# Attention vectors spread by TensorE from 2 KB rows, a plan that knows the transfers' rate, leads by group, aggregates copied by ScalarE

## Chip, core and metric

The kernel runs on one core of one Trainium2 chip. The metric is the device time of one execution in microseconds; it is given as the median of several executions. The program computes everything in float32.

## What is computed

128 graphs of 128 nodes with 256 features each pass through three graph-attention layers and one gated graph layer. Before each of the four, the features are normalized per node and cut at zero; the layer's result is added to the features.

```python
h = jnp.maximum(_layernorm(x, axis=-1), 0.0)
# attention layer (three times, own W and a)
Wh = jnp.einsum('bnf,fo->bno', h, W)
e = (Wh @ a1)[:, :, None] + (Wh @ a2)[:, None, :]
e = jnp.where(e > 0, e, ALPHA * e)
attention = jax.nn.softmax(jnp.where(adj > 0, e, NEG_BIG), axis=-1)
x = x + jax.nn.elu(jnp.einsum('bij,bjo->bio', attention, Wh))   # the third times nodemask
# gated layer, three steps
m = jnp.einsum('bnd,de->bne', h, weight[i])
aggr = jnp.einsum('bst,bsd->btd', A, m)
h = _gru_cell(aggr, h, w_ih, w_hh, b_ih, b_hh)                  # r, z, n gates of 256 each
```

## The kernel before

**Groups.** The graphs are worked on in 33 groups: a first and a last one of two graphs, and 31 of four (`SIZES`). For each group `gat(g)` does the three attention layers and `gru(g, ...)` the three gated steps. Names carry the group, then the layer or step, then the half: `ahp_2_1_0` is group 2, second attention layer.

**The plan.** Nothing is issued while the Python code runs through the groups. Each call of `add(engine, cost, rank, fn, ...)` notes an operation with an estimate of its cost; `load` notes a DMA on SP. `Plan.issue` then schedules all of them on paper: at each turn it takes the operation that can start first by the estimates (among those within 0.1 us the one of the lowest rank), and no operation whose rank is more than 6 above the lowest unfinished one. The order so found is the order in which every engine's queue holds its instructions. Each engine works through its queue in this order, so an instruction that has to wait holds up all behind it. Before the change, each load has one number, `lands`, for the time from its issue to its landing, whatever else is in flight.

**Ranks.** Group g's gated steps have ranks 3g, 3g + 1 and 3g + 2; its attention layers begin at 3g - lead(g) and are 2 apart. `lead` decides how far ahead of its gated steps a group's attention is worked on: 8.5 for the first two groups (`FAR = 2`), 6.5 for all others.

**Setup.** `attention_weights` folds a layer's vector `a` into its matrix: DVE multiplies each row of `w` with `a` and sums (L294), TensorE transposes the sums to all partitions (`vp`, L299), ScalarE copies them (`va`, L306). For this, `a` must lie in all 128 partitions: `ab` is loaded by a DMA that reads the 2 KB 128 times (L287). `transposed` loads and turns the GRU's weights (`whh`, `wih`, `gt`), and `combined` multiplies them (`wcp`).

**An attention layer** (`attention`): statistics on DVE (`st`, `mv`), the root on POOL (`rs`), the normed features on ScalarE (`xn`), scores on DVE (`scr`, L505), masked sums `em` (L547), exponentials on ScalarE (L565), then the weights are turned (`atp` by TensorE for groups 0 and 1; through DRAM, `tr_at`, `d_at`, `at`, for the others, which also spread the second score through DRAM, `de`, `er`). TensorE multiplies: `ahp` (L617, 16 records of 128 columns for four graphs), copied to `ah` (L624), then `hp` (L636, 16 records of 256). The result goes by `t` (L650) and two DVE operations into `xo` (L652, L654).

**A gated step** (`step` in `gru`): TensorE makes the aggregate `agp` (L803) in two halves, from the node-major state `hn` and the adjacency `am`. A copy `ag` (L811, on DVE) brings each half to SBUF; the one PSUM bank of the tag `tr` is free again after it. The products `nn`, `r`, `z`, `ni` (all L780) read the state `h` and the weights `whh`, or `ag` and the combined weights `wc`. ScalarE makes `wn`, `r`, `n`, `z` (L833 to L853), DVE the new state `h` (L841 to L870). For groups 2 to 30 the state is brought into node-major form for the next step by a DVE transpose of 32 x 32 blocks, a store to DRAM and four loads (`tr_hn`, `d_hn`, `hn`); the other groups use TensorE transposes (`hnp`, L752). All groups but the first get their first `h` from the normed features `hn0` by such a transpose, store and loads (`tr_h`, `d_h`, `h`), and all but the last two bring their last state back so (`tr_o`, `d_o`, `o`).

A product of 512 columns in float32 stands in the profile as two records.

Of the kernel before, what the change touches and what calls it, by code (L numbers as in the profile page):

```python
# [39 lines left out]
class Plan:  # L40
# [12 lines left out]
    def val(self, pool, tag, bufs, make):  # L53
        return Val(self.rings.setdefault((id(pool), tag), [[None] * bufs, 0]), make)

    def load(self, lands, rank, fn, **keys):

        op = self.add("SP", 0.45, rank, fn, **keys)
        op.lands = lands
        return op  # L60

    def add(self, engine, cost, rank, fn, reads=(), writes=(), after=(), takes=()):
# [45 lines left out]
    def issue(self):  # L108
        waits_for = {op: len(op.deps) for op in self.ops}
        uses = {}  # L110
        for op in self.ops:
            for v in op.vals:
                uses[v] = uses.get(v, 0) + 1
        by_rank = sorted(self.ops, key=lambda op: op.rank)
        engines = sorted({op.engine for op in self.ops})
        ready, free = {e: [] for e in engines}, {e: 0.0 for e in engines}
        held = [op for op in self.ops if not op.deps]
        best, changed, low, order = {}, set(engines), 0, []

        def start(op):  # L120
            t = max(free[op.engine], op.ready)
            for v in op.vals:
                if not v.taken:
                    slots, n = v.ring
                    old = slots[n % len(slots)]
                    if old is not None:
                        if uses[old]:
                            return None
                        t = max(t, *(o.end + self.lag(o, op.engine, False) for o in old.ops))
            return t  # L130

        def choose(engine):
            found = [(start(op), op) for op in ready[engine]]
            found = [f for f in found if f[0] is not None]
            if not found:
                return None
            first = min(t for t, _ in found)
            soon = [(op.rank, t, i) for i, (t, op) in enumerate(found) if t <= first + self.WINDOW]
            _, t, i = min(soon)
            return t, found[i][1]  # L140

        while len(order) < len(self.ops):
            while by_rank[low].end is not None:
                low += 1
            limit = by_rank[low].rank + self.AHEAD
            for op in held:
                if op.rank <= limit:
                    ready[op.engine].append(op)
                    changed.add(op.engine)
            held = [op for op in held if op.rank > limit]  # L150
            for e in sorted(changed):
                best[e] = choose(e)
            changed = set()
            open_ = {e: best[e] for e in engines if best[e] is not None}
            assert open_, "the plan is stuck"
            e = min(open_, key=lambda e: open_[e][0])
            t, op = open_[e]
            ready[e].remove(op)
            op.end = free[e] = t + op.cost
            order.append(op)  # L160
            changed.add(e)
            for v in op.vals:
                uses[v] -= 1
                if not v.taken:
                    slots, n = v.ring
                    slots[n % len(slots)], v.ring[1], v.taken = v, n + 1, True
                    changed.update(engines)
                if not uses[v]:
                    changed.update(engines)
            for u in op.users:  # L170
                u.ready = max(u.ready, op.end + self.lag(op, u.engine, u.deps[op]))
                waits_for[u] -= 1
                if not waits_for[u]:
                    held.append(u)
        for op in order:
            for v in op.vals:
                v.t
            op.fn()
# [3 lines left out]
def kernel(  # L182
# [85 lines left out]

    ident = const.tile([P, P], FT, name="ident")
    make_identity(nc, ident)  # L270
    mhalf = const.tile([P, G], FT, name="mhalf")
    nc.vector.memset(mhalf, -0.5)

# [6 lines left out]
    def attention_weights(l, w, a):  # L280
        rank = 1.5 * l - 8.0
        wt, va = const_val(f"w_{l}", [KD, D]), const_val(f"va_{l}", [2, D])
        first = l - 11.2
        load(4.0, first, lambda: nc.sync.dma_start(
            wt.t, w.rearrange("(k p) o -> p k o", p=P)), writes=[wt])
        ab = val(su, "ab", [2, D], f"ab_{l}")
        load(4.0, first, lambda: nc.sync.dma_start(  # L287
            ab.t, bass.AP(tensor=a.tensor, offset=a.offset, ap=[[0, P], [1, 2 * D]])), writes=[ab])
        wa = val(su, "wa", [2, KD], f"wa_{l}")
        vp = bank("gat", f"vp_{l}")  # L290

        def one(s, k):
            scr = val(su, "scr", [D], f"scr_{l}_{k}_{s}")
            add("DVE", dve(D) + 0.08, rank, lambda: nc.vector.scalar_tensor_tensor(  # L294
                scr.t, wt.t[:, k, :], 1.0, ab.t[:, s, :], op0=OP.mult, op1=OP.mult,
                accum_out=wa.t[:, s, k : k + 1],
            ), reads=[wt, ab], writes=[scr, (wa, (s, k))])
            c = s * KD + k
            add("PE", 0.11, rank, lambda: nc.tensor.transpose(  # L299
                vp.t[:, c * P : (c + 1) * P], wa.t[:, s, k : k + 1].to_broadcast([P, P]), ident  # L300
            ), reads=[(wa, (s, k))], writes=[(vp, c)])

        for s in range(2):
            for k in range(KD):
                one(s, k)
        add("ACT", act(T), rank, lambda: nc.scalar.copy(  # L306
            va.t.rearrange("p s d -> p (s d)"), vp.t), reads=[vp], writes=[va])
        W.append(wt)
        VA.append(va)
# [6 lines left out]
    def mask():  # L316
        nm = val(su, "nm", [N], "nm")
        nmp = bank("gat", "nmp")
        load(8.0, SETUP, lambda: nc.sync.dma_start(nm.t[:B], nodemask), writes=[nm])
        add("PE", 0.11, SETUP, lambda: nc.tensor.transpose(nmp.t[:, :B], nm.t[:B], ident[:B, :B]),  # L320
            reads=[nm], writes=[nmp])
        add("ACT", act(P), SETUP, lambda: nc.scalar.copy(nmT.t, nmp.t[:, :B]),
# [5 lines left out]
    def transposed(src, dst, name):  # L328
        rows = src.shape[0] // P
        ld = val(su, "wld", [O3 // P, D], f"{name}_ld")  # L330
        load(8.0 if rows > KD else 4.0, SETUP, lambda: nc.sync.dma_start(
            ld.t[:, :rows], src.rearrange("(r p) d -> p r d", p=P)), writes=[ld])

        def part(k, r0, n):
# [53 lines left out]
    def load_bias(dst, src):  # L388
        def fn():
            with nc.allow_non_contiguous_dma(reason="768 biases, once"):  # L390
                nc.sync.dma_start(dst.t, src.rearrange("(c p) -> p c", p=P))
        add("SP", 0.8, SETUP, fn, writes=[dst])

    load_bias(bi, b_ih)
    load_bias(bh, b_hh)
# [32 lines left out]
    def exchanged(srcs, cut, dst, name, n, rank):  # L428
# [16 lines left out]

        for k in range(kd):
            blocks(k)
        load(2.8 if kd == 1 else 3.8, rank, lambda: nc.sync.dma_start(
            d.t.rearrange("q r j f -> (q r) j f"), tr.t[:, :, :f]), reads=[tr], writes=[d])

        def back(j):
            load(2.8 if kd == 1 else 3.8, rank, lambda: nc.sync.dma_start(
                dst.t[j * 32 : (j + 1) * 32, :, :f], d.t[:, :, j, :].rearrange("q r f -> r q f")
            ), reads=[d], writes=[(dst, j)])

# [3 lines left out]
    def turned_state(src, dst, name, n, rank):  # L459
# [6 lines left out]
        add("DVE", dve(n * P), rank, lambda: nc.vector.transpose(  # L466
            tr.t.rearrange("p b j -> p (b j)"), src.t[:, : n * P]
        ), reads=[src], writes=[tr], takes=[d, dst])
        load(2.6, rank, lambda: nc.sync.dma_start(d.t.rearrange("b p f -> p b f"), tr.t),
            reads=[tr], writes=[d])  # L470

        def back(j):
            load(2.8, rank, lambda: nc.sync.dma_start(
                dst.t[j * 32 : (j + 1) * 32, : n * P].rearrange("c (m r) -> c m r", r=32),
                d.t[:, :, j * 32 : (j + 1) * 32].rearrange("b (q c) r -> c (b q) r", q=Q),
            ), reads=[d], writes=[(dst, j)])
# [4 lines left out]
    def attention(g, l, xt, cap, xo):  # L481
# [40 lines left out]
        if far:  # L522
# [1 line left out]
                dram, f"de{n}", 2, lambda: dram.tile([P, n], FT, tag=f"de{n}", name=f"de_{name}")  # L524
            )
            er = val(gw, "er", [N * G], f"er_{name}")
            load(2.2, rank, lambda: nc.sync.dma_start(de.t, e.t[:, 1, :n]),
                reads=[(e, (1, b)) for b in range(n)], writes=[de], takes=[er, em])
            load(4.6, rank, lambda: nc.sync.dma_start(
                er.t[:, : N * n], de.t.rearrange("p n -> (p n)").partition_broadcast(P)  # L530
            ), reads=[de], writes=[er])
        else:
            e2 = bank("gat", f"e2_{name}")

# [125 lines left out]
    def gat(g):  # L660
# [3 lines left out]
        adj_t = val(grp, "adj", [G, N], f"adj_{g}", dtype=I32, cut=n)  # L664
        cap = val(grp, "cap", [G, N], f"cap_{g}", cut=n)
        am = val(grp, "am", [G, N], f"am_{g}", bufs=4, cut=n)
        load(4.8, rank - 4, lambda: nc.sync.dma_start(
            x0.t, x[b0 : b0 + n].rearrange("b n d -> n b d")), writes=[x0])
        load(4.8, rank - 3.6, lambda: nc.sync.dma_start(
            adj_t.t, adj[b0 : b0 + n].rearrange("b i j -> i b j")), writes=[adj_t])  # L670
        add("DVE", 0.42, rank, lambda: nc.vector.tensor_scalar(
            cap.t, adj_t.t, 0.0, 2.0 * BIG, op0=OP.is_gt, op1=OP.mult), reads=[adj_t], writes=[cap])
# [53 lines left out]
    def gru(g, xt, am, hn0, h0):  # L726
# [36 lines left out]
        def step(i):  # L763
# [22 lines left out]
            def aggregate(k):  # L786
# [21 lines left out]

                for b in range(n_g):
                    part(b)  # L810
                add("DVE", dve(TG), quick, lambda: nc.vector.tensor_copy(t.t[:, :TG], ps.t[:, :TG]),  # L811
                    reads=[ps], writes=[t])

            def half(c):
# [92 lines left out]

        for k in range(KD):
            result(k)
        load(2.6, rank, lambda: nc.sync.dma_start(  # L910
            out[b0 : b0 + n_g].rearrange("b n d -> n b d"), xt.t), reads=[xt])

    URGENT = 2.0

    def lead(g):

        return 8.5 if g < FAR else 6.5

    for g in range(NG):
        gru(g, *gat(g))  # L920
# [37 lines left out]
```

## Time and profile before

| What | Before |
|---|---|
| median of 3 runs | 2776.41 us (2775.74 to 2777.18) |
| profiled execution, whole | 2774.5 us |
| its span, first to last instruction | 2772.7 us |
| mean granted TensorE clock | 0.995 |
| TensorE (PE) busy | 2710.1 us, 98% |
| VectorE (DVE) busy | 2199.0 us, 79% |
| ScalarE (ACT) busy | 1171.7 us, 42% |
| DVE copies of aggregates (L811) | 198, of 128 x 512 mostly, 676 ns |
| loads of `ab` | 3, 256 KB each, 5.3 us to landing (first 16 us) |

In the profile's lines a group shows the line, the engine, the operation, the tiles as out<-in, the number of instructions, and after a bar busy time and mean duration. A wait shows who waited for whom, the total, the number of times and the longest. A row of the timeline shows its start and length in microseconds, and in brackets how long the engine was idle before it and who ended that. The granted clock is the share of TensorE's full clock that the chip allowed. SPq is SP's queue of DMA issues. An end of several waits is put down to the last of them.

### The profile page before, as it was taken

The page shows a single profiled execution, that of the slowest core. Times are in us where ns is not written, and L with a number is a line of the kernel's source. Part 1 is how long each engine was busy: PE and PEld are TensorE (multiplying, and loading weights), DVE is VectorE, ACT ScalarE, POOL GpSimd, SP SyncE. Part 2 cuts the span into 40 slices and gives each one's busy share as a digit, 9 for nine tenths or more (in the row PEclk, how much of TensorE's full clock was granted, in tenths as well). Part 3 has the DMA queues.
Part 4 walks back from the last instruction along what each step waited for, and adds up shares of the span by engine and source line. Part 5 has one row for each costly group of instructions (what it writes and reads, how often), then busy time and mean ns, then how long its engine had stood idle before and what let it go on. Part 6 is the DMA issues. An engine that isn't in the chain of part 4 may idle for free.

```text
span 2772.7 us, 32377 instructions
## 1 busy us (share of the span) xinstructions
PE 2710.1 (98%) x9557; PEld 1565.2 (56%) x9557; DVE 2199.0 (79%) x5738; ACT 1171.7 (42%) x2511; POOL 288.2 (10%) x369
## 2 busy tenths in 40 slices
PE   6998999999999999999999999999999999999998
PEld 4755555555555555555555555555555555555546
DVE  7778888887888878887888878788788887888644
ACT  4444444443444444443444444444344444444322
POOL 2101011010101010101011101011101010101000
PEclk9999999999999999999999999999999999999999
DMA  3213234333334323334333334333333333333310
GB/s 102 57 44 103 77 94 110 103 86 92 89 93 111 105 75 99 91 92 111 97 83 96 95 92 107 103 84 91 88 100 103 104 87 88 80 94 93 78 44 12
DMA packets 503519, 246.08 MB, mean 89 GB/s; under 512 B 280624, under 2 KB 472112, under 8 KB 503344
## 3 DMA queue, kind: packets, MB, share of 16 engines
q1 hardware_dynamic: 503344, 244.03, 33.6%
q8 instruction: 76, 1.25, 0.2%
q14 instruction: 99, 0.81, 0.1%
HBM read 140.06 MB, written 103.87 MB: 88 GB/s over the span
## 4 chain that ended last, share of the span: by engine, by line
PE 84%; DVE 11%; ACT 2%; DMA 1%; issue 1%; SPq 0%; POOL 0%; ACTq 0%; DVEq 0%; POOLq 0%
PE r L780 21%; PE z L780 21%; PE ni L780 11%; PE hp L636 10%; PE nn L780 9%; PE ahp L617 6%; PE agp L803 5%; DVE em L547 2%; DVE xo L652 1%; DVE xo L654 1%; ACT em L565 1%; DVE ag L811 1%; DVE d L867 1%; DVE h L870 1%; DVE d L863 1%
## 5 line engine op out<-in xcount | busy, mean ns | idle before, releaser
L780 PE MATMUL nn<-h,whh 128*128 128x512 f32 (+1 forms) x792 | 396.3, 582 | 11.2 <-DMA h<-d_h 9.0
L780 PE MATMUL r<-ag,wc 128*128 128x512 f32 (+1 forms) x792 | 394.5, 581 | 8.4 <-DVE ag L811 8.4
L780 PE MATMUL r<-h,whh 128*128 128x512 f32 (+1 forms) x792 | 395.2, 580 | 0.0
L780 PE MATMUL z<-h,whh 128*128 128x512 f32 (+1 forms) x792 | 394.3, 579 | 0.0
L780 PE MATMUL z<-ag,wc 128*128 128x512 f32 (+1 forms) x792 | 394.1, 579 | 0.0
L780 PE MATMUL ni<-ag,wc 128*128 128x512 f32 (+1 forms) x792 | 394.0, 579 | 0.0
L636 PE MATMUL hp<-w,ah 128*128 128x256 f32 x1536 | 360.5, 380 | 2.5 <-ACT ah L624 2.4
L636 PEld LDWEIGHTS hp<-w,ah 128*128 128x128 f32 x1536 | 290.5, 191 | 100.7 <-issue 61.5
L841 DVE SCALAR_TENSOR_TENSOR n<-r,wn 128x512 f32<-128x512 f32 (+1 forms) x198 | 133.6, 675 | 224.8 <-ACT r L838 222.9
L505 DVE SCALAR_TENSOR_TENSOR scr<-xn,va 128x256 f32<-128x256 f32 x732 | 268.6, 419 | 32.4 <-ACT xn L497 32.2
L833 ACT ACTIVATE wn<-nn,bh 128x512 f32<-128x512 f32 (+1 forms) x198 | 132.9, 671 | 359.1 <-PE nn L780 358.9
L838 ACT ACTIVATE r<-r,brz 128x512 f32<-128x512 f32 (+1 forms) x198 | 132.8, 671 | 351.8 <-PE r L780 351.5
L803 PEld LDWEIGHTS agp<-am,hn 128*128 128x128 f32 x1536 | 201.1, 191 | 88.3 <-issue 64.1
L780 PEld LDWEIGHTS r<-ag,wc 128*128 128x128 f32 x792 | 148.3, 190 | 176.4 <-issue 145.8
L780 PEld LDWEIGHTS z<-h,whh 128*128 128x128 f32 x792 | 150.1, 190 | 170.9 <-issue 161.5
L565 ACT ACTIVATE em<-em,nmx 128x128 f32<-128x128 f32 x384 | 149.3, 390 | 228.3 <-DVE nmx L561 228.3
L780 PEld LDWEIGHTS z<-ag,wc 128*128 128x128 f32 x792 | 148.3, 190 | 159.4 <-issue 157.4
L780 PEld LDWEIGHTS r<-h,whh 128*128 128x128 f32 x792 | 147.8, 191 | 159.7 <-issue 155.0
L780 PEld LDWEIGHTS ni<-ag,wc 128*128 128x128 f32 x792 | 146.7, 190 | 154.5 <-issue 137.1
L617 PEld LDWEIGHTS ahp<-at,xn 128*128 128x128 f32 x1536 | 188.8, 194 | 47.6 <-issue 42.1
L803 PE MATMUL agp<-am,hn 128*128 128x128 f32 x1536 | 205.9, 276 | 8.7 <-ACT hn L792 4.4
L780 PEld LDWEIGHTS nn<-h,whh 128*128 128x128 f32 x792 | 138.5, 191 | 103.8 <-issue 95.0
(91 smaller groups left out, 3401.9 us busy)
## 6 DMA issues: line engine op xcount, KB each, us to landing
d_hn<-tr_hn SPq DMA_DIRECT2D x116, 256.0 KB, 2.3
hn<-d_hn SPq DMA_DIRECT2D x464, 64.0 KB, 2.4
er<-de SPq DMA_DIRECT2D x90, 256.0 KB, 3.8
d_at<-tr_at SPq DMA_DIRECT2D x90, 256.0 KB, 2.0
at<-d_at SPq DMA_DIRECT2D x360, 64.0 KB, 2.0
x<-in_x_dram SPq DMA_DIRECT2D x31, 512.0 KB, 4.0
d_h<-tr_h SPq DMA_DIRECT2D x31, 512.0 KB, 3.0
h<-d_h SPq DMA_DIRECT2D x124, 128.0 KB, 3.2
```

The costliest lines, as they stand in the source:

```text
L505: add("DVE", dve(D), rank, lambda: nc.vector.scalar_tensor_tensor(scr.t, xn.t[:, b, :], 1.0 if far else rs.t[:, b : b + 1], VA[l].t[:, s, ...
L547: add("DVE", dve(P) + (0.15 if far else 0.05), rank, lambda: nc.vector.scalar_tensor_tensor(em.t[:, b, :], e2_row(b), e.t[:, 0, b : b + 1] ...
L565: add("ACT", 0.42, rank, lambda: nc.scalar.activation(em.t[:, b, :], em.t[:, b, :], AF.Exp, bias=nmx.t[:, b : b + 1], accum_out=sm.t[:, b ...
L617: add("PE", pe(P), rank, lambda: nc.tensor.matmul(summed(ps, b), xn.t[:, b, k * P : (k + 1) * P], turned_weights(b), start=True, stop=True ...
L636: add("PE", pe(D), rank, lambda: nc.tensor.matmul(hp.t[:, b * D : (b + 1) * D], ah.t[:, k, c * P : (c + 1) * P], W[l].t[:, k, :], start=(k ...
L652: add("DVE", dve(T), rank, lambda: nc.vector.scalar_tensor_tensor(u(), hp.t, 0.0, u(), op0=OP.max, op1=OP.add), reads=[hp, *parts], writes ...
L654: add("DVE", dve(T), rank, lambda: nc.vector.scalar_tensor_tensor(u(), t.t, 1.0, u(), op0=OP.min, op1=OP.add), reads=[t, *parts], writes=p ...
L780: nc.tensor.matmul(o, w.t[:, k, c * P : (c + 1) * P], m, start=start, stop=stop)
L803: nc.tensor.matmul(ps.t[:, b * P : (b + 1) * P], s, am.t[:, b, :], start=True, stop=True)
L833: add("ACT", act(TG) + 0.1, quick, lambda: nc.scalar.activation(wn.t[:, :TG], nn.t[:, :TG], AF.Identity, bias=bh.t[:, cn : cn + 1]), reads ...
L838: add("ACT", act(TG) + 0.1, quick, lambda: nc.scalar.activation(r.t[:, :TG], pr.t[:, :TG], AF.Tanh, bias=brz.t[:, cr : cr + 1], scale=0.5) ...
L841: add("DVE", dve(TG), quick, lambda: nc.vector.scalar_tensor_tensor(n.t[:, :TG], r.t[:, :TG], 1.0, wn.t[:, :TG], op0=OP.add, op1=OP.mult), ...
```

## The change

There are four parts.

1. The attention vector `a` is loaded as one row of 2 KB into one partition (`ar`). TensorE spreads it to all partitions with a matrix product of a row of ones and this row, into the PSUM bank `ab` of the tag `gat`, and DVE reads it there.
2. In the plan, a load has a size in KB in place of a landing time. The plan keeps the time `moved` until which the loads before occupy the transfers, at 250 KB per us; a load lands 1.9 us after its bytes are through (plus `more` for the two kinds with many small pieces). The biases, which before had the default landing of 2.6 us, are counted too.
3. `lead` takes its values for groups 0 to 4 from a list; from group 5 on it stays 6.5.
4. The copies `ag` of the aggregates are done by ScalarE in place of DVE.

```diff
-    def load(self, lands, rank, fn, **keys):
+    def load(self, kb, rank, fn, more=0.0, **keys):
         op = self.add("SP", 0.45, rank, fn, **keys)
-        op.lands = lands
+        op.kb, op.more = kb, more
...
             op.end = free[e] = t + op.cost
+            if e == "SP":
+                moved = max(moved, op.end) + op.kb / 250.0
+                op.lands = moved - op.end + 1.9 + op.more
...
+    ones = const.tile([1, P], FT, name="ones")
+    nc.vector.memset(ones, 1.0)
...
-        ab = val(su, "ab", [2, D], f"ab_{l}")
-        load(4.0, first, lambda: nc.sync.dma_start(
-            ab.t, bass.AP(tensor=a.tensor, offset=a.offset, ap=[[0, P], [1, 2 * D]])), writes=[ab])
+        ar = val(su, "ar", [2 * D], f"ar_{l}")
+        load(2, first - 0.1, lambda: nc.sync.dma_start(
+            ar.t[:1, :], a.rearrange("n o -> o n")), writes=[ar])
+        ab = bank("gat", f"ab_{l}")
+        add("PE", pe(T), rank, lambda: nc.tensor.matmul(
+            ab.t, ones[:1, :], ar.t[:1, :], start=True, stop=True), reads=[ar], writes=[ab])
...
-                scr.t, wt.t[:, k, :], 1.0, ab.t[:, s, :], op0=OP.mult, op1=OP.mult,
+                scr.t, wt.t[:, k, :], 1.0, ab.t[:, s * D : (s + 1) * D], op0=OP.mult, op1=OP.mult,
...
-        load(2.6, rank, lambda: nc.sync.dma_start(d.t.rearrange("b p f -> p b f"), tr.t),
+        load(64 * n, rank, lambda: nc.sync.dma_start(d.t.rearrange("b p f -> p b f"), tr.t),
...
-                add("DVE", dve(TG), quick, lambda: nc.vector.tensor_copy(t.t[:, :TG], ps.t[:, :TG]),
+                add("ACT", act(TG), quick, lambda: nc.scalar.copy(t.t[:, :TG], ps.t[:, :TG]),
                     reads=[ps], writes=[t])
...
+    LEADS = [9.0, 9.5, 7.0, 6.5, 7.0]
     def lead(g):
-        return 8.5 if g < FAR else 6.5
+        return LEADS[g] if g < len(LEADS) else 6.5
```

The other loads get their sizes in the same way: 256 for `w`, 128n for `x`, 64n for `adj`, 128 per 128 rows of the weights, 64n and four times 16n for a turned state and the turned weights (twice that for `h` and `o`), 2 for `de`, 64n for `er` with 1.6 more, 4 for each bias with 3.0 more.

More of the change, by code (lines that the diff above doesn't have):

```diff
@@ L117, in issue @@
         held = [op for op in self.ops if not op.deps]
+        moved = 0.0
         best, changed, low, order = {}, set(engines), 0, []
@@ L283, in attention_weights @@
         first = l - 11.2
-        load(4.0, first, lambda: nc.sync.dma_start(
+        load(256, first, lambda: nc.sync.dma_start(
             wt.t, w.rearrange("(k p) o -> p k o", p=P)), writes=[wt])
-        ab = val(su, "ab", [2, D], f"ab_{l}")
-        load(4.0, first, lambda: nc.sync.dma_start(
-            ab.t, bass.AP(tensor=a.tensor, offset=a.offset, ap=[[0, P], [1, 2 * D]])), writes=[ab])
+        ar = val(su, "ar", [2 * D], f"ar_{l}")
[4 more added lines that the diff above has]
+            ab.t, ones[:1, :], ar.t[:1, :], start=True, stop=True), reads=[ar], writes=[ab])
         wa = val(su, "wa", [2, KD], f"wa_{l}")
@@ L318, in mask @@
         nmp = bank("gat", "nmp")
-        load(8.0, SETUP, lambda: nc.sync.dma_start(nm.t[:B], nodemask), writes=[nm])
+        load(64, SETUP, lambda: nc.sync.dma_start(nm.t[:B], nodemask), writes=[nm])
         add("PE", 0.11, SETUP, lambda: nc.tensor.transpose(nmp.t[:, :B], nm.t[:B], ident[:B, :B]),
@@ L330, in transposed @@
         ld = val(su, "wld", [O3 // P, D], f"{name}_ld")
-        load(8.0 if rows > KD else 4.0, SETUP, lambda: nc.sync.dma_start(
+        load(128 * rows, SETUP, lambda: nc.sync.dma_start(
             ld.t[:, :rows], src.rearrange("(r p) d -> p r d", p=P)), writes=[ld])
@@ L391, in fn @@
                 nc.sync.dma_start(dst.t, src.rearrange("(c p) -> p c", p=P))
-        add("SP", 0.8, SETUP, fn, writes=[dst])
+        load(4, SETUP, fn, more=3.0, writes=[dst])
     load_bias(bi, b_ih)
@@ L447, in exchanged @@
             blocks(k)
-        load(2.8 if kd == 1 else 3.8, rank, lambda: nc.sync.dma_start(
+        load(64 * kd * n, rank, lambda: nc.sync.dma_start(
             d.t.rearrange("q r j f -> (q r) j f"), tr.t[:, :, :f]), reads=[tr], writes=[d])
         def back(j):
-            load(2.8 if kd == 1 else 3.8, rank, lambda: nc.sync.dma_start(
+            load(16 * kd * n, rank, lambda: nc.sync.dma_start(
                 dst.t[j * 32 : (j + 1) * 32, :, :f], d.t[:, :, j, :].rearrange("q r f -> r q f")
@@ L468, in turned_state @@
         ), reads=[src], writes=[tr], takes=[d, dst])
-        load(2.6, rank, lambda: nc.sync.dma_start(d.t.rearrange("b p f -> p b f"), tr.t),
+        load(64 * n, rank, lambda: nc.sync.dma_start(d.t.rearrange("b p f -> p b f"), tr.t),
             reads=[tr], writes=[d])
         def back(j):
-            load(2.8, rank, lambda: nc.sync.dma_start(
+            load(16 * n, rank, lambda: nc.sync.dma_start(
                 dst.t[j * 32 : (j + 1) * 32, : n * P].rearrange("c (m r) -> c m r", r=32),
@@ L526, in attention @@
             er = val(gw, "er", [N * G], f"er_{name}")
-            load(2.2, rank, lambda: nc.sync.dma_start(de.t, e.t[:, 1, :n]),
+            load(2, rank, lambda: nc.sync.dma_start(de.t, e.t[:, 1, :n]),
                 reads=[(e, (1, b)) for b in range(n)], writes=[de], takes=[er, em])
-            load(4.6, rank, lambda: nc.sync.dma_start(
+            load(64 * n, rank, lambda: nc.sync.dma_start(
                 er.t[:, : N * n], de.t.rearrange("p n -> (p n)").partition_broadcast(P)
-            ), reads=[de], writes=[er])
+            ), more=1.6, reads=[de], writes=[er])
         else:
@@ L666, in gat @@
         am = val(grp, "am", [G, N], f"am_{g}", bufs=4, cut=n)
-        load(4.8, rank - 4, lambda: nc.sync.dma_start(
+        load(128 * n, rank - 4, lambda: nc.sync.dma_start(
             x0.t, x[b0 : b0 + n].rearrange("b n d -> n b d")), writes=[x0])
-        load(4.8, rank - 3.6, lambda: nc.sync.dma_start(
+        load(64 * n, rank - 3.6, lambda: nc.sync.dma_start(
             adj_t.t, adj[b0 : b0 + n].rearrange("b i j -> i b j")), writes=[adj_t])
@@ L909, in gru @@
             result(k)
-        load(2.6, rank, lambda: nc.sync.dma_start(
+        load(128 * n_g, rank, lambda: nc.sync.dma_start(
             out[b0 : b0 + n_g].rearrange("b n d -> n b d"), xt.t), reads=[xt])
     URGENT = 2.0
+    LEADS = [9.0, 9.5, 7.0, 6.5, 7.0]
     def lead(g):
-        return 8.5 if g < FAR else 6.5
+        return LEADS[g] if g < len(LEADS) else 6.5
     for g in range(NG):
```

## The prediction

> **What bounds the kernel now.** I read the engines' shares first, then TensorE's waits, then the stretches of the start, then single waits in the timeline. From the page:
>
> ```profile
> PE 2710.1 (98%) x9557; PEld 1565.2 (56%) x9557; DVE 2199.0 (79%) x5738; ACT 1171.7 (42%) x2511; POOL 288.2 (10%) x369
> PE   6998999999999999999999999999999999999998
> ```
>
> TensorE is the bound. So I count in lost time: wall time less the queued work at full rate. Start to start in the timeline, a product of 512 columns takes 0.859 us (two records), of 384 0.646, of 256 0.431, of 128 0.223, a transpose 0.109. With 2232, 24, 912, 1536 and 149 of them that is 1917.3 + 15.5 + 393.1 + 342.5 + 16.2 = 2684.6 us. The span of 2772.7 therefore holds 88.1 us lost, and only these can be won. Where they lie, by stretches (time, then busy time of PE, PEld, DVE, ACT, POOL, granted clock, DMA share, GB/s):
>
> ```profile
> 58.90:62.30 3.40, 1.25 (x8) 0.87 (x6) 3.25 (x11) 0.60 (x1) 0.09 (x1) 1.00 0.01 2
> 62.30:72.50 10.20, 5.12 (x22) 4.65 (x23) 6.55 (x24) 4.19 (x13) 2.21 (x4) 0.50 0.01 2
> 229.50:239.80 10.30, 3.70 (x5) 1.67 (x6) 7.00 (x29) 2.08 (x4) 2.01 (x3) 0.50 0.68 184
> 300.00:2580.00 2280.00, 2270.08 (x7873) 1288.22 (x7872) 1863.61 (x4819) 977.45 (x2080) 241.58 (x299) 1.00 0.36 94
> ```
>
> Two stretches at half clock, each after a long wait, and a middle that is full. At the first GRU product of group 1 (128.5 us, 90.3 us of work done) 38.2 us are lost; at that of group 2 (236.1, 180.2) 55.9; from there to 300 about 4.0, from 300 to 2580 17.3, in the last groups 10.9. TensorE's waits (waiter, releaser: us in total, times, longest):
>
> ```profile
> PE nn L780 <- DMA h<-d_h: 9.0, 2, 8.4
> PE r L780 <- DVE ag L811: 8.4, 14, 0.8
> PE vp L299 <- DVE scr L294: 8.2, 1, 8.2
> PE atp L589 <- DVE nm L687: 6.9, 1, 6.9
> PE agp L803 <- DVE ag L811: 2.8, 4, 1.3
> ```
>
> Each part of the change meets one of these.
>
> **Part 1, the attention vectors.** The first DVE product waits for the 256 KB spread, and the transposes of w_hh wait for their load behind it:
>
> ```profile
> 7.61 0.42 DVE L294 SCALAR_TENSOR_TENSOR scr<-w,ab 128x256 f32<-128x256 f32 x1 [2.77 <-DMA ab<-in_L_gnn_a_dram]
> 14.68 1.54 PE L338 MATMUL whh<-ident,whh_ld 128*128 128x128 f32 x6 [1.66 <-DMA whh_ld<-in_L_gnn_w_hh_dram]
> ```
>
> Three spreads go; two of them (512 KB) stand ahead of w_hh on the queue. At 258 GB/s (mean of the first 16 us) to 360 (the plateau) that is 1.4 to 2.0 us. The first spread landed at 7.50, w_0 at 5.31, so DVE may start up to 2.2 us sooner. Added: three TensorE products of 512 columns, 3 x 0.859 = 2.6 us of work (twice that at half clock), in a stretch where TensorE is busy 43.9 of 60 us; two go ahead of the first transposes, the third stands between w_hh and group 0's first aggregate, on the path. I take 1.7 us sooner up to the end of group 1's second layer (76.7 us now, 42.6 of work, 34.1 lost), bounds 0 and 3. There the changed order has queued 45.2, so it has lost 75.0 - 45.2 = 29.8. The work total becomes 2687.2.
>
> **Part 2, leads and rates.** The leads of groups 0 to 4 go from 8.5, 8.5, 6.5, 6.5, 6.5 to 9, 9.5, 7, 6.5, 7. What matters is the cover: the work that TensorE has in its queue between a result and the instruction that needs what comes of it. I count it from the order in which both programs queue it.
>
> Group 1, layer 2 to 3: the cover shrinks from 19.9 us to 12.1, since group 0's GRU products now stand behind. The way from hp through DVE, ACT and back took 21.5 us (76.7 to 98.2). In the changed order DVE has nine 256-column GRU steps fewer inside it, 9 x 0.42 = 3.8, so about 18: a new wait of 6 us, at most 9.4. A wait of that kind stands in the trace, where the transposes of group 1's second layer follow their scores directly:
>
> ```profile
> 67.09 1.08 PE L589 MATMUL atp<-ident,em 128*128 128x128 f32 x4 [6.94 <-DVE nm L687]
> ```
>
> (nm L687 only came last; the scaled em, L576, ended just before it, at 66.95.) It was followed by 10.2 us at clock 0.50 with 5.1 us of work in them, that is 2.6 lost besides. I take 2.5 for the new one (bounds 1.7 and 5), 1.5 for small waits of group 0's short steps. Stretch to group 1's first product: now 4.1 lost, then 10. Total there 39.8 (now 38.2).
>
> The Trainium skill ("TensorE: Matmul & The Clock Gate", Part 1) says that an idle window of about 3.4 us halves the array's clock and that a busy one of as long is needed to return. It speaks against opening this wait; by it alone the loss would be 1.7 us, by the row above 2.6.
>
> Group 2, last layer to GRU: the cover grows from 9.6 us to 20.3. This is the longest wait of all:
>
> ```profile
> 225.65 0.42 SPq L448 DMA_DIRECT2D d_h<-tr_h  x1
> 231.60 1.73 SPq L452 DMA_DIRECT2D h<-d_h  x4
> 236.10 1.19 PE L780 MATMUL nn<-h,whh 128*128 128x512 f32 x1 [8.43 <-DMA h<-d_h]
> ```
>
> From the last hp (212.0) to 236.1 the way took 24.1 us. In it the spill took 5.9 us against a median of 3.0, beside the o loads, which now come behind on SP's queue; three of group 1's GRU steps stood between the statistics on DVE. Nearest to the new case is a way of 19 to 24; I take 21.5, a wait of 1.2 instead of 8.6. The stretch from group 1's first product to group 2's loses 17.7 now (besides: 1.9, 2.6 and 1.3 at 216 to 227, and small ones). I leave 2.3 for the two hn copies of group 1, 1.2, and 2 for what may come: 5.5. Lost at group 2's first product: 45.3 instead of 55.9, bounds 40 and 54. After it the half-clock loss of 1.9 goes, but two aggregates (groups 2 and 3, second step) are used with no cover, 0.95 each: even.
>
> The new rates change only numbers in the plan. SP issues the same loads, one row for each spread, and x, adj and biases in another order; from 300 to 2580 us no wait of TensorE ends on one of those.
>
> **Part 3, copies on ScalarE.** In the middle every wait over 0.2 us but one is a copy that came late: per four groups (333.9 us) 0.66 + 0.93 + 0.26, and 0.3 to refill behind them, of 2.8 lost. It isn't the copy's length but DVE's queue:
>
> ```profile
> ACT r L838 <- PE r L780: 351.5, 151, 6.9
> DVE ag L811 <- PE agp L803: 48.1, 24, 4.9
> ```
>
> ScalarE stood idle until TensorE's result at 151 of 198 r, DVE at only 24 of 198 ag: elsewhere DVE was still at something else. Between agp's last matmul and the copy lie 0.31 us at best and 0.54 more on average; ScalarE's wn, r, z and ah come 0.02 to 0.14 late. Nor is the copy longer: 512 columns PSUM to SBUF take ScalarE 585 ns (L624), DVE 676 (L811).
>
> What is queued behind it: ScalarE is in order, so a copy behind four exponentials (0.45 each) or hn (0.52) waits for DVE's chain too, and r, z and wn stand behind a copy that waits for agp. 198 copies x 0.585 = 116 us bring ScalarE to 46%; DVE falls to 75%.
>
> In the changed order most copies have 1.72 us of cover or more, as now; one group in three has two with 0.86 and 0.89. There 0.31 + 0.585 + about 0.15 to the reader is 0.1 to 0.3 more than the cover. So 0.4 per three groups, and 0.16 per group of other small waits as now: 27.3 groups x 0.29 = 8 us instead of 17.3. Bounds 4 (no waits at all but refills) and 30 (below).
>
> **Sum.** 45.3 + 4.0 + 8 + 10.9 = 68.2 lost, + 2687.2 = 2755.4, 17.3 less than the span. The profiled execution took 2774.5 in all, 1.9 under the median of the runs, 2776.41: 2757.2 for its like, 2759 for the median. The bound of a measurable change is 0.2%, 5.6 us: faster below 2770.9, slower above 2782.0.
>
> **Rivals.**
> *The wait only moves.* Group 1's wait is 9.4, its half clock costs 5, and group 2's way takes 24.1: 5.9 + 2.6 more lost, + 1.5 with part 1 at a gain of 0.2. Then 2759 + 10 = 2769. For it: two waits of 7 and 8 us stand there today in just such chains. Against: group 2's cover doubles. 0.16.
> *The copies are no sooner.* ScalarE's queue holds them up as DVE's did, the middle stays at 17.3: 2768. For it: hn and exponentials stand ahead of several copies. Against: the idle rows above. 0.12.
> *The turned state comes late (slower).* The way from the last z to the turned hn: 0.26 + 0.69 (z), 2 x 0.72 (DVE), 0.74 (transpose), 2.3 (spill), 1.7 (four issues), landing 1.8, 2.4 or 5.3 (least, median, most): 8.9, 9.5, 12.4 us. Today's cover for a step's second half is 12 to 13.8; in two of three groups, going into the third step, it becomes 11.2. If the way takes 13.2 there, 2.0 x 2/3 x 27.3 = 36 more: 2795. It turns the sign from 12.5 us on (1.26 a time). Against: one wait of 0.3 us at hn in the whole trace, and z, d, h and the transpose now follow each other with nothing between. 0.11.
>
> **Numbers.** My case: 0.61, 2759, its own range 2746 to 2766. The range of all reaches down by smaller losses in part 2 (5) and the middle (4) and up over the first two rivals, to 2778. Faster: 0.61 + 0.11 of the first rival + 0.10 of the second = 0.82; no change 0.07; slower 0.11.
>
> **What would show it.** Right: clock 0.50 after a wait at about 90 us on atp or ahp of group 1, none near 230; "nn <- DMA h" under 4 us; "r <- ag" under 4 us in all; vp's first wait near 7 us. Wrong: agp waiting for hn in the middle, ScalarE's r and z starting late, or group 1's new wait above 10 us.

## The result, and the profile after

The changed kernel takes 2757.69 us (median of four runs, 2756.84 to 2758.13), the kernel before 2776.07 (2773.93 to 2777.18) beside it: a ratio of 0.9935, 95% interval 0.992 to 0.9951, 18.4 us less. Its profiled execution took 2757.7 us with a span of 2756.0.

From the page of the changed kernel (line numbers are some 10 higher now):

```profile
PE 2712.8 (98%) x9563; PEld 1569.7 (57%) x9563; DVE 2082.3 (76%) x5541; ACT 1280.4 (46%) x2709; POOL 293.7 (11%) x369
PE   7899999999999999999999999999999999999998
```

DVE is busy 117 us less, ScalarE 109 more, and TensorE is the bound as before. The stretches, with the columns of before:

```profile
95.10:96.60 1.50, 0.63 (x4) 0.42 (x4) 1.50 (x5) 0.00 (x0) 0.00 (x0) 0.86 0.00 0
96.60:98.00 1.40, 1.32 (x6) 1.32 (x7) 1.40 (x6) 0.00 (x0) 0.00 (x0) 0.50 0.00 0
215.00:240.00 25.00, 25.00 (x75) 12.69 (x74) 20.55 (x62) 12.45 (x27) 2.51 (x3) 1.00 0.37 111
300.00:2580.00 2280.00, 2276.18 (x7893) 1294.27 (x7892) 1776.66 (x4679) 1071.83 (x2241) 248.49 (x302) 1.00 0.36 94
```

The clock is at 0.50 behind a wait near 95 us and no longer near 230, where TensorE is now busy throughout. In the middle it is busy 6 us more of the same 2280. TensorE's waits, and one row of ScalarE's:

```profile
PE atp L599 <- DVE em L586: 6.9, 2, 3.6
PE agp L813 <- DMA hn<-d_hn: 2.5, 3, 1.1
PE nn L790 <- DVE h L880: 1.9, 4, 1.2
PE r L790 <- ACT ag L821: 1.3, 7, 0.2
PE vp L309 <- DVE scr L304: 1.1, 1, 1.1
ACT ag L821 <- PE agp L813: 262.8, 147, 4.4
```

The wait of nn on the DMA of h (9.0 us before) is gone, r waits 1.3 for its aggregate instead of 8.4, and ScalarE stands idle until TensorE's result at 147 of 198 copies, where DVE did at 24. The waits on the scaled sums `em` have grown from one of 1.4 us to 6.9 in two. These two places, and the first product of group 2, in the timeline:

```profile
56.57 0.66 PE L599 MATMUL atp<-ident,em 128*128 128x128 f32 x2 [3.22 <-DVE em L586]
95.17 0.63 PE L599 MATMUL atp<-ident,em 128*128 128x128 f32 x4 [3.63 <-DVE em L586]
225.86 1.02 PE L790 MATMUL nn<-h,whh 128*128 128x512 f32 x2
```

The first is group 0's third layer, which nobody had waited for so long; the second group 1's, the wait that the prediction opened. The third row has no bracket: there is no wait. One of the signs that were to speak against the prediction shows faintly: agp waits three times for the turned state `hn` (2.5 us in all, 0.3 before), at 296 us in group 2, at 1351 in group 15 and at 2627 in group 30.

In lost time, counted as in the prediction (wall time less queued work), with a second profiled execution of the changed kernel from the last experiment:

| Mark | before | predicted | changed | again |
|---|---|---|---|---|
| end of group 1's second layer | 34.1 | 29.8 | 34.6 | 34.0 |
| group 1's first gated product | 38.2 | 39.8 | 42.2 | 41.5 |
| group 2's first gated product | 55.9 | 45.3 | 44.0 | 43.1 |
| group 3's | 60.1 | | 48.1 | 46.7 |
| group 30's | 76.0 | | 55.6 | 54.7 |
| end of the span | 88.1 | 68.2 | 68.8 | 67.2 |

### The profile page after: what moved, and what is told of

It reads as the page before. It is cut to its first block, busy times and chain, and to the rows that moved or that the text cites. A ratio compares the mean times of both kernels' runs of the same rounds, so it can differ in the third digit from the quotient of the medians.

```text
span 2756.0 us, 32248 instructions
## 1 busy us (share of the span) xinstructions
PE 2712.8 (98%) x9563; PEld 1569.7 (57%) x9563; DVE 2082.3 (76%) x5541; ACT 1280.4 (46%) x2709; POOL 293.7 (11%) x369
## 3 DMA queue, kind: packets, MB, share of 16 engines
q8 instruction: 76, 1.25, 0.2%
## 4 chain that ended last, share of the span: by engine, by line
PE 88%; DVE 8%; ACT 2%; DMA 1%; issue 1%; POOL 0%; SPq 0%; DVEq 0%; ACTq 0%; POOLq 0%
PE z L790 21%; PE r L790 21%; PE hp L646 11%; PE ni L790 11%; PE nn L790 10%; PE ahp L627 6%; PE agp L813 5%; DVE em L557 1%; DVE scr L515 1%; DVE xo L662 1%; DVE xo L664 1%; DVE d L877 1%; ACT em L575 1%; DVE h L880 1%; DVE n L856 0%
## 5 line engine op out<-in xcount | busy, mean ns | idle before, releaser
L646 PE MATMUL hp<-w,ah 128*128 128x256 f32 x1536 | 373.2, 381 | 0.5 <-ACT ah L634 0.2
L821 ACT COPY ag<-agp 128x512 f32<-128x512 f32 (+1 forms) x198 | 113.0, 571 | 263.2 <-PE agp L813 262.8
L526 POOL TENSOR_SCALAR xo<-xo 128x1024 f32<-128x1024 f32 (+1 forms) x66 | 73.2, 1110 | 1215.6 <-DVE xo L664 989.8
```

The costliest lines, as they stand in the source:

```text
L526: add("POOL", 0.14 + n * D / 1070, rank, lambda: nc.gpsimd.tensor_scalar(xo.t, xt.t, 1.0, -1.0, op0=OP.mult, op1=OP.add), reads=[xt], writ ...
L646: add("PE", pe(D), rank, lambda: nc.tensor.matmul(hp.t[:, b * D : (b + 1) * D], ah.t[:, k, c * P : (c + 1) * P], W[l].t[:, k, :], start=(k ...
L821: add("ACT", act(TG), quick, lambda: nc.scalar.copy(t.t[:, :TG], ps.t[:, :TG]), reads=[ps], writes=[t])
```

## The experiments

| Run | median us | ratio to before, 95% interval |
|---|---|---|
| e1, copies alone | 2759.5 | 0.9943, 0.993 to 0.9955 |
| e2, all but the copies | 2784.2 | 1.0034, 1.0022 to 1.0047 |
| e3, old leads | 2776.3 | 1.0003, 0.9994 to 1.0012 |
| e4, old spread | 2755.3 | 0.9928, 0.9915 to 0.994 |
| e5, leads alone | 2768.4 | 0.9974, 0.9966 to 0.9983 |
| e6, leads and copies | 2752.0 | 0.9917, 0.9903 to 0.993 |
| e7, other leads | 2757.0 | 0.9933, 0.992 to 0.9945 |
| e8, short covers | 2886.7 | 1.041, 1.0391 to 1.0428 |
| e9, no spread, copies costed as DVE's | 2759.8 | 0.9938, 0.9925 to 0.995 |
| e10, the same with the spread | 2762.8 | 0.9952, 0.9939 to 0.9964 |
| e11, old landing times | 2765.4 | 0.996, 0.9946 to 0.9973 |
| e12, the changed kernel again | 2758.6 | 0.9937, 0.9924 to 0.9949 |

The kernel before took 2775.2, 2775.0 and 2776.8 beside the three sets of four.

**The copies, with the order held.** The first two runs move only the engine that executes a copy; the plan still costs it where it was, so no other instruction changes its place.

```diff
 # e1, on the kernel before
-add("DVE", dve(TG), quick, lambda: nc.vector.tensor_copy(t.t[:, :TG], ps.t[:, :TG]),
+add("DVE", dve(TG), quick, lambda: nc.scalar.copy(t.t[:, :TG], ps.t[:, :TG]),
 # e2, on the changed kernel
-add("ACT", act(TG), quick, lambda: nc.scalar.copy(t.t[:, :TG], ps.t[:, :TG]),
+add("ACT", act(TG), quick, lambda: nc.vector.tensor_copy(t.t[:, :TG], ps.t[:, :TG]),
```

> The kernel before, its order on every queue unchanged, but the 198 copies of aggregates are done by ScalarE. Theory (VectorE's queue held the copies up): from 300 to 2580 us TensorE loses 7 to 9 us instead of 17.3, its waits on ag (r and agp on ag, 11.2 us in all now) fall under 3, the whole gains 10 (8 to 12): 2766 against 2776. The start up to 300 us stays within 2 us. Rival (the order of the new plan did it, the engine of the copy does not matter): 2774 to 2778, waits on ag as before.

> The changed kernel, its order on every other queue unchanged, but the copies of aggregates are back on VectorE. Theory (VectorE's queue): every copy is late by the 0.5 us of before, so the middle loses the 10 us again; and the two copies in three groups with 0.86 and 0.89 us of cover come 0.31 + 0.68 + 0.54 - 0.87 = 0.66 late, 18 times, 12 us more: 2776, bounds 2767 (the 10 alone) and 2780. Rival (the order did it): 2757 to 2760.

e1 gained 15.7 us, half as much again as expected and beyond the range, and its middle lost less than the 7 to 9 us of the theory. This middle, and after it that of e2, as stretches, each with the whole execution's rows on the copies:

```profile
300.00:2580.00 2280.00, 2279.68 (x7916) 1297.38 (x7915) 1787.94 (x4681) 1078.06 (x2253) 247.37 (x302) 1.00 0.36 94
ACT ag L811 <- PE agp L803: 271.0, 155, 3.8
```

```profile
300.00:2580.00 2280.00, 2262.51 (x7832) 1281.92 (x7831) 1840.78 (x4786) 967.81 (x2060) 246.91 (x299) 1.00 0.36 94
DVE ag L821 <- PE agp L813: 77.8, 29, 5.4
PE r L790 <- DVE ag L821: 11.0, 17, 0.9
```

TensorE has 0.3 us idle in 2280 in e1, 17.5 in e2, 3.8 in the changed kernel. Summed over the instructions' late starts, the middle loses 1.1 us in e1, 7.5 in the changed kernel, 16.1 in the kernel before (by the prediction's way of counting 17.3) and 30.1 in e2; the 29 expected there was right, but e2's start lost 5 more besides, and its 2784.2 lies above the range. In the middle a copy on DVE begins 0.54 us (before) and 0.53 (e2) later on average than the earliest one behind its matmul; on ScalarE 0.02 (e1) and 0.07 (changed). Both runs refute the order as the cause and speak for DVE's queue. They do not part it from two smaller effects of the same move: the copy itself is 0.09 us shorter on ScalarE (585 ns against 680, medians), and DVE's other work is relieved of the copies. They also show that the changed order gives back 6.4 us of what the copies bring: in e1 every copy of the middle has 1.72 us of cover or more, in the changed kernel 17 of the 100 in the second and third steps of groups 5 to 29 have 0.86 to 1.3, and r's waits at the eight with 0.86, 3.3 us with the refill, are the largest item of its 7.5.

**The leads.**

```diff
 # e3, on the changed kernel
-    LEADS = [9.0, 9.5, 7.0, 6.5, 7.0]
+    LEADS = [8.5, 8.5]
 # e5, on the kernel before
+    LEADS = [9.0, 9.5, 7.0, 6.5, 7.0]
...
-        return 8.5 if g < FAR else 6.5
+        return LEADS[g] if g < len(LEADS) else 6.5
```

> The changed kernel with the old leads (8.5 for groups 0 and 1, 6.5 for all others). In the order that the plan then gives, the cover of group 1's second attention layer up to the third grows from 12.1 to 17.9 us, that of group 2's last layer up to its first gated product shrinks from 20.7 to 10.9. Theory (a wait is way less cover): group 1's way took 15.7 us, its wait and half clock of 4.9 us go; group 2's way took 20.2 (24.1 in the kernel before), so a wait of 9 to 13 and 2.6 of half clock come: 7 to 11 slower, 2765 to 2769. Rival (leads move waits about, and the way shortens with the work that stands in it): 2757 to 2760.

> The kernel before with the new list of leads and nothing else. Its order gives group 1's third layer a cover of 12.1 us (before 19.9) and group 2's first gated product 21.8 (before 9.6). Theory (a wait is way less cover): group 1 loses some 4 us more, group 2 some 12 to 14 less at its first gated product, the middle loses its 17 us unchanged: 9 us less in all, 2766 (2763 to 2769). Rival (the long ways are long because VectorE has the copies, so leads alone bring little): 2771 to 2777.

e3 lost the whole gain of the change, 18.6 us (its profiled execution 15.6), about twice what was expected; both theories missed. One row of its timeline:

```profile
236.62 2.05 PE L790 MATMUL nn<-h,whh 128*128 128x512 f32 x2 [8.90 <-DMA h<-d_h]
```

Group 1's wait went (36.4 lost at its third layer's first product hp, 40.8 in the changed kernel), and group 2's came back with its half clock: 53.8 lost at its first product in place of 44.0, both as the covers say. The rest lies behind: to group 5's first product 10.1 are lost (5.6), among them one more aggregate without cover, 1.0 for a turned state and 2.1 for the one bank `tr` that a copy had not yet freed; from there to group 30's 8.3 (6.0). e5 gained 6.6 us, inside its range, but not by the parts foretold: 46.1 are lost at group 1's first product, 8 more than before and not 4. The stretch from there to group 2's first product lost 12.9 less, as expected, which leaves 51.0 there (55.9 before). Its middle lost about as much as before.

**Rates.**

```diff
 # e11, on the changed kernel: load() takes the fixed landing times again
-        op.kb, op.more = kb, more
+        op.lands = lands
...
-                moved = max(moved, op.end) + op.kb / 250.0
-                op.lands = moved - op.end + 1.9 + op.more
...
-        load(256, first, lambda: nc.sync.dma_start(
+        load(4.0, first, lambda: nc.sync.dma_start(
...
```

> The changed kernel with the old fixed landing times of the loads in the plan; spread, leads and copies as changed. The order then gives group 2's first gated product a cover of 11.3 us (20.3 in the changed kernel) and, in the middle, 8 copies of 100 with 0.9 to 1.1 us in place of 17. Theory (the rates act through the covers): group 2 waits 9 to 12 more and 2.6 of half clock, the middle loses 3 less: 2757.7 + 9 to 12, 2767 to 2770. Rival (the rates only change numbers in the plan): 2756 to 2759.

e11 took some 7 us more than the changed kernel, a little under the range. Its profiled execution, 2770.5, is 5 us above the four others. In it 56.8 us are lost at group 2's first product. They are not one wait but pieces on the same way (1.7 for the normed features, 0.8 for the first copy, 2.5 for h) with the clock at half twice. So the rates do work, by the cover that the order then gives to group 2. Without the spread they are not needed for it: e6, with neither, has a cover of 21.8 there.

**Leads and copies without the other two parts.** e6 is e1 with the new list of leads, e7 the same with `[9.5, 9.0, 7.0, 7.0, 6.5]`, e8 with `[9.5, 9.0, 7.0, 6.5, 7.0]`.

> The kernel before with the new leads and the copies of aggregates by ScalarE at their old places in the order; no rates, no spread by TensorE. Every copy in the middle has 1.72 us of cover or more. Theory: the start of the changed kernel (42 to 45 us lost at group 2's first gated product) and the middle of the run with the copies alone (1 us lost from group 5 to 30): 54.6 us lost at the end against 66.0 in that run, so 11 us less than its 2759.5: 2748 (2746 to 2752), faster than the changed kernel. Rival (without rates and spread the gains don't add): 2757 or more.

> As the run with leads and copies, but leads 9.5, 9, 7, 7, 6.5. Group 1's third layer then has a cover of 16.4 us in place of 12.1, group 1's first gated product 25.2 (29.9), group 2's 19.0 (21.8). Theory: group 1's way of 15.7 is covered, 3 to 4 us and the half clock behind it go, group 2 waits 1 to 2: 2746 (2744 to 2749). Rival (with a group 0 step back inside it the way grows with its cover, and the wait stays or moves to group 2): 2748 to 2752.

> As the run with the leads 9.5, 9, 7, 7, 6.5, but with 6.5 and 7 for groups 3 and 4. From there on the order repeats with each group instead of each four, and the cover from a step's last product to the aggregate that needs the turned state is 10.3 to 12.9 us for all halves, 25 groups long, where the other order has 12 to 18. This is the third rival's place. In the changed kernel's trace that way took 8 to 9.5 us where it went straight through (second halves into the third step) and 11 to 13 elsewhere. If the way is 11.5 whatever the cover, 0.5 to 1.2 us are missing some 75 times: 40 to 90 us slower, 2790 to 2835. If the way goes straight through whenever it is needed (9.3): 2745 to 2750, as the other.

e6 is the fastest kernel of the study, 2750.7 to 2753.4 us, with its median at the edge of its range: 65.0 us lost at the end of the span, 23.1 less than before, although 50.3 are lost at group 2's first product where 42 to 45 were expected. From group 3's first product to group 30's it loses 1.6 us, the changed kernel 7.5.

e7 missed by 11 us. Group 1's way did as foretold (from its second layer's hp to its third's 4.1 us are lost, 7.4 in e6), but the new order lost 2 more ahead of it, 3 more in the first step of group 2 and 2 in the middle.

e8 missed on the far side, 4.1% slower than before. From its waits:

```profile
PE nn L780 <- DVE h L870: 61.5, 57, 1.9
PE agp L803 <- DMA hn<-d_hn: 40.4, 33, 1.9
```

The way from a step's last product to the landing of the turned state took 11.4 to 14.9 us there in groups 5 to 28, mostly with less than 1 us to spare or none, against covers of 10.3 to 12.9. So it does not go straight through when it is needed. In the changed kernel the covers are 11.2 and more, and where they are 11.2 (17 of 100) the way mostly took 8 to 9.5. The expectation had overlooked a second short cover: in 25 places the new state itself has 3.5 us, everywhere else over 4.2; its waits (nn on h, 61.5) are the larger part.

**The spread.**

```diff
 # e4, on the changed kernel; e9 and e10 differ by the same lines
-        ar = val(su, "ar", [2 * D], f"ar_{l}")
-        load(2, first - 0.1, lambda: nc.sync.dma_start(
-            ar.t[:1, :], a.rearrange("n o -> o n")), writes=[ar])
-        ab = bank("gat", f"ab_{l}")
-        add("PE", pe(T), rank, lambda: nc.tensor.matmul(
-            ab.t, ones[:1, :], ar.t[:1, :], start=True, stop=True), reads=[ar], writes=[ab])
+        ab = val(su, "ab", [2, D], f"ab_{l}")
+        load(256, first, lambda: nc.sync.dma_start(
+            ab.t, bass.AP(tensor=a.tensor, offset=a.offset, ap=[[0, P], [1, 2 * D]])), writes=[ab])
...
```

Both e9 and e10 have the leads `[9.0, 9.5, 7.0, 7.0, 7.0]` and the copies on ScalarE, costed in the plan as DVE's.

> The changed kernel with the old 256 KB loads of the attention vectors and without the three products that spread them; leads, rates and copies as changed. Covers of the two long ways as in the changed kernel (12.1 and 20.7). Theory 1 (the prediction's term: the spread by TensorE brings 1.7 us up to the end of group 1's second layer): that point 1.7 later, 2759.5. Theory 2 (read from the two traces: the changed kernel lost 3.3 us less up to 46 us, but its third layer of group 0 began 2.3 later, since 5 us more work stands ahead of the second layer's product, and the gain went into a wait there): the end of group 1's second layer comes at 76 us again instead of 79.5, and the whole 3 us sooner, 2754.5.

> The changed kernel with the old 256 KB loads of the attention vectors, leads 9, 9.5, 7, 7, 7, and the copies of aggregates on ScalarE but costed in the plan as work of VectorE. That order gives every copy in the middle 1.72 us of cover or more, the turned state 12.1 or more, and the start of the run with the old spread (covers 12.1 and 20.3). Theory (start and middle add, each set by its covers): 48.5 us lost at group 3's first gated product (50 in the run with the old spread, less the aggregates without cover), 6.5 from there to the end as in the run with leads and copies: 55 lost, 2749 (2747 to 2752), faster than the changed kernel by 6 to 10. Rival (the middle's loss sits with the leads or the rates, not with the copies' covers): 2754 to 2758.

> The same as the run without spread, but the attention vectors are spread by TensorE from the 2 KB rows. All covers behind the setup are equal, so the pair prices the first part of the change alone. Theory 1 (the prediction's term): 1.7 us sooner than its pair, 2747. Theory 2 (the 2.6 us of TensorE work and the order that comes with them eat the earlier start): 2 us (1 to 3) later than its pair, 2751.

> The changed kernel itself, on the chip of these runs, as their yardstick: 2757.7 (2756 to 2759).

Without the spread e4 is 2.4 us below the changed kernel (2755.1 to 2756.1 against 2756.2 to 2762.9 in nine runs), e9 3.0 below e10, where single runs overlap. The end of group 1's second layer comes at 79.8, 79.2, 80.5 and 81.1 us in four executions with the spread (changed, e12, e10, e2) and at 79.7 and 77.2 in e4 and e9. So e4's whole time is that of its second theory, but the point that was to come at 76 us came where the changed kernel has it; where the 2.4 us arise is not shown. Two executions of one order differ by up to 2.5 us there, so the price is about 2 us with an uncertainty of the same size; a gain of 1.7 fits neither pair.

e9 itself missed its 2749 by 11, and e10 its 2751 by 12. The middle of e9 lost 0.8 us from 480 to 2560, as wanted, but from group 2's first product to group 5's 13.4 are lost (e6: 2.8). The longest wait there stands at a cover that had not been counted, that of the turned weights of group 4's first layer, in its timeline:

```profile
244.40 1.83 PE L623 MATMUL ahp<-at,xn 128*128 128x128 f32 x7 [3.41 <-DMA at<-d_at]
```

From 246 to 256 us the clock stands at 0.78. That this list of leads brought groups 3 and 4 too close together is what the trace suggests; it was not tried apart.

## Why the prediction was right, and where it wasn't

The time and the whole sum hold (68.2 us lost predicted, 68.8 found), but that they meet so closely is luck, as the terms show:

- **Part 1, mis-sized, and by the two pairs above in its sign.** It should have brought 1.7 us up to the end of group 1's second layer (75.0 us); that point came at 79.8 instead of 76.7. Not all of this is the change: e1, whose order on TensorE is that of the kernel before, has 78.3 there. The first step is as foretold: vp's first wait ends at 6.8 instead of 8.2, the transposes of w_hh begin 1.7 sooner, and at 46 us the change has lost 3.2 less. The step that failed is to carry this on to the end of the chain. With the spread the plan puts 24.4 us of work ahead of the product hp of group 0's second layer instead of 19.4. It begins 1.7 later (40.5; but e1 has 40.3 by the old order), and TensorE, with 35.8 us of work behind it ahead of the third layer's weights instead of 33.3, gives the gain back in the wait of 3.2 at 56.6. This wait is the steadiest sign: 3.22 us in all four executions with the spread, 1.38 in the kernel before and e1, 0.09 in e4 and e9. Where a chain through several engines sets the end, a TensorE that is ahead in work is not ahead in time.
- **Part 2, group 1.** From there to group 1's first product 10 us were to be lost, 7.6 were. By the prediction's measure (end of hp to the first ahp) the way took 16.8 us (79.8 to 96.7), not 18. The waits were 3.6 and another 0.9 on `at`, 4.5 in place of 6, and the half clock lasted 3.4 us.
- **Part 2, group 2.** The way to its first product was 20.2 us with a cover of 20.3 (21.5 was taken): no wait. The stretch lost 1.8 instead of 5.5.
- **Part 3.** The middle lost 7.5 us (8 predicted), and for the reasons given: prompt copies, short waits, of 0.2, at the cover of 0.86 (the other, 0.89, needed none).
- **What it left out.** "The new rates change only numbers in the plan" is true of the instructions and false of the time: without them group 2's cover is 11.3, and some 7 us are gone (e11). The sum did not suffer, as it counted its covers in the order that the rates had made. And e1 shows that the old order would have taken the copies' gain almost whole.
- **Rivals.** The wait that only moves did not come: no wait of group 1 reached 9.4. Copies no sooner: refuted by e1 and e2. The turned state came late three times, 2.5 us in all, not in every third group. But e8 shows that this rival stands one lead away: 0.5 more or less in the leads of groups 3 and 4 is all that parts it from e7, and the late turned state and the late state together cost 130 us.

The errors nearly cancel: 4.8 too little lost up to group 1's second layer, 2.4 and 3.7 too much in the two stretches behind it, 1.9 too little from group 2 to the end.

Two rules of the Trainium skill bear on this. "Perfetto Trace Analysis", in Optimizing Scalar/DVE Operations, says that offloading work from DVE to ScalarE may make sense if DVE is saturated. Here DVE was busy 79%, and the offload brought 15.7 us (e1) all the same: what counted was that a copy began 0.54 us late in DVE's queue, though DVE was not full. "TensorE: Matmul & The Clock Gate", Part 1, has the clock halved after an idle window of about 3.4 us. The wait of 3.63 at 95 us agrees; e7, below, does not need so long a wait (2.16 us).

## What to carry to other kernels

In a kernel whose order is planned, first move an operation between engines with the order held, and change the order apart: here the copies brought 15.7 us alone, and the new order then gave 6 of them back in the middle. Count, for every result that another engine or a DMA brings back, the work that the bound engine has in its queue until it needs it, and compare that with the way in the trace; a step is safe only when all of these covers are counted, since a small number in the plan's ranks (0.5 of a lead) moved them by some 2 us in every group from e7 to e8. A faster start of the bound engine was worth nothing here, where a chain over other engines set the end.

Where both kernels are beaten, it is by leaving out: e6, with leads and copies alone, took 2752.0, a ratio of 0.9917 (0.9903 to 0.993) beside 0.9935 and 0.9937 of the changed kernel; its runs do not overlap with those of the changed kernel, the intervals of the ratios just do.

## What was not expected of the hardware

The clock can fall to half behind a wait that is well under 3 us. In e7 TensorE was idle for 0.68 and 2.16 us with 1.2 us of work between them. In the timeline:

```profile
226.64 1.16 PE L803 MATMUL agp<-am,hn 128*128 128x128 f32 x8 [0.68 <-ACT ag L811]
229.96 1.10 PE L780 MATMUL nn<-h,whh 128*128 128x512 f32 x2 [2.16 <-DMA h<-d_h]
```

and in the stretches behind, with the granted clock in the third column from the end:

```profile
230.00:232.00 2.00, 2.00 (x4) 1.01 (x5) 1.93 (x6) 0.07 (x1) 0.00 (x0) 0.74 0.00 0
232.00:234.00 2.00, 2.00 (x3) 0.67 (x3) 1.59 (x7) 1.86 (x9) 1.27 (x2) 0.50 0.15 61
```

In e6 the same two places were idle for 0.68 and 1.50 us, and the clock stayed at 1.00:

```profile
227.84 1.16 PE L803 MATMUL agp<-am,hn 128*128 128x128 f32 x8 [0.68 <-ACT ag L811]
230.50 1.10 PE L780 MATMUL nn<-h,whh 128*128 128x512 f32 x2 [1.50 <-DMA h<-d_h]
```

The traces tell more of where the limit lies. In all fourteen, the granted clock changes only at whole multiples of 3.41 us from the start of its first recorded stretch, so each trace can be cut into stretches of 3.41 us. The one that ends with e7's fall (227.56 to 230.97) holds the whole wait of 2.16 and has TensorE busy for 1.25 us; the 0.68 lies ahead of it. The one in e6 that holds the wait of 1.50 (228.10 to 231.51) has 1.91 us.

From 300 to 2580 us the clock falls nine times in the fourteen traces, eight of them in e8, where no wait of TensorE is longer than 1.9 us. Each fall ends a stretch with 1.39 to 1.65 us busy, and every stretch that leaves the clock up has 1.63 or more. So in this part of the kernel it was a stretch busy for less than about half that went with a fall, not a single long wait. Ahead of 300 us this does not hold throughout: in e3 the clock falls at 226 us behind a stretch that is busy for 2.35 us. No run was made to test it.
